# An LSTM whose input part per step comes from DRAM as three bfloat16 rows instead of from SBUF in float32

## The chip, the cores and the metric

The kernel runs on one core of one Trainium2 chip. A core has five engines that run side by side and wait for each other through semaphores: TensorE (PE; its weight loads are listed apart as PEld), VectorE (DVE), ScalarE (ACT), GpSimd (POOL) and SyncE (SP), which here only issues transfers. The metric is the time of one execution on the device, in microseconds (us); lower is better.

## The reference

The input is x, 1250 rows of 512 floats, with 20000 edges (src, dst) between the rows. Two blocks are added to it:

```
x = x + gnn(layernorm(x), src, dst)          # two graph layers with 512x512 weights
x = x + lstm(layernorm(x))                   # one sequence of 1250 steps, hidden size 512

# lstm, for each row t:
combined = concat(x_t, h)                    # 1024
f, i, o  = sigmoid(combined @ W_f + b_f), ...(W_i), ...(W_o)
c        = f * c + i * tanh(combined @ W_c + b_c)
h        = o * tanh(c)
```

The graph layer sums neighbours' rows by dst, scales by the degrees, and multiplies with two weights. The product of x_t with the upper half of the four gate weights does not depend on h, so it can be done for all rows ahead of the recurrence; this is the "input part" of the gates, 2048 numbers per row. The product with h must be done step by step.

## The kernel before, in words

**Stretches.** The 1250 rows are cut into 32 stretches of 40 rows (`P, LEN = 32, 40`), which run side by side. Each stretch starts 90 steps early (`WARM = 90`) with a zero state on the rows that come before it, so that the loop has 130 steps instead of 1250, with 32 rows in each. At the end the kernel compares the state at the end of every stretch with that at the start of the next one, and falls back on a strictly sequential loop (`in_order`) if they differ; with these inputs it doesn't. `EARLY = 3` is how many stretches back the warm-up reaches.

**Tiles.** Rows lie in ten tiles of 128 partitions: tile i holds rows 4i to 4i+3 of all 32 stretches, partition 4p+q being row 4i+q of stretch p. `chunks` and `order` say in which order the tiles are worked on in the graph layers (tiles 8, 9, then 0 to 3, then 4 to 7).

**Stages.** (1) Layer norm, the first linear layer, and the count of the edges into an adjacency matrix, to 205 us. (2) `fast()` starts after a branch: it loads the input half of the gate weights (`load_wx`, 32 KB per partition, in a pool `late_w` at the right end of the SBUF), then `layers()` runs the two graph layers. Their float32 features are written as a sum of three bfloat16 planes (`split`: ACT copies to bfloat16, DVE subtracts, ACT copies the rest, DVE subtracts), which go through TensorE as bfloat16 (line 682). Before the first layer `with_identity` (line 165) scales both layers' weights. (3) `load_wh` loads the recurrent half of the gate weights, then `gate_inputs` (line 497) is called for the ten tiles: DVE normalises the tile's rows (line 499), TensorE transposes them (line 151), ACT copies the transposes (line 156), TensorE does four products of 128x512 (line 505, j = 0 to 3), and DVE adds the bias and writes the result, float32, to SBUF (line 507). `xw_tile(i)` says where: in buffers of the layers that are free by then (`adj`, `planes`, `h`, `base1`). (4) `lstm()` runs the 130 steps.

**A step.** The gates of the 32 stretches lie in two PSUM tiles (s = 0, 1; each has half of the hidden units of every 128-block), with partition 32j+p for block j of stretch p. `open_gates` (line 528) writes the input part into them: for each s and j one product of a selection matrix `sel` with 32 columns and the tile's 128 rows; the columns of `sel` pick row q of every stretch, shifted by e stretches in the warm-up. `add_gates` (line 536) adds the recurrent products, 32 of them, in an order that is written out by hand:

```
for b, s in ((0, 0), (1, 0), (0, 1), (2, 0), (3, 0), (1, 1), (2, 1), (3, 1)):
```

Blocks b = 0, 1 need the state of half 0 (`hT0`), blocks 2, 3 that of half 1. A float32 product is two matmul instructions in the trace, and the four column groups j run side by side on the array. `cell` (line 540) follows for s = 0 and s = 1: three ACT instructions (lines 543, 545, 547), two DVE (549, 550), ACT (552), DVE (553), and a DVE transpose (554) which makes the new `hT` of that half.

**What sets the order of the work.** Pools of buffers and a planner: the planner orders the instructions of each engine, DMA issues on SP and POOL too, from estimated times, and an instruction of a later part of the program can stand ahead of one of an earlier part. In the blocks under `manual_schedule` PE, DVE and ACT keep the written order; SP and POOL stay with the planner. In each engine the order is then fixed, and an instruction that waits holds up all behind it. Buffers of closed pools are used again, and what is written there first waits for the last use before.

**Transfers around the steps.** `x2c` is a copy of the rows in the order of the steps, 40 transfers of 64 KB (line 759, half on SP and half on POOL), in a buffer that is free only after stage 3. In the last 40 steps POOL adds the output of the step to it (line 781), and `store` (line 717) writes it out, in six groups, on SP.

Of the kernel before, what the change touches and what calls it, by code (L numbers as in the profile page):

```python
# [9 lines left out]
F32 = mybir.dt.float32  # L10
F16 = mybir.dt.float16
BF16 = mybir.dt.bfloat16
# [26 lines left out]
def gnn_lstm_kernel(  # L39
# [63 lines left out]
    WARM = 90  # L103
    EARLY = -(-WARM // LEN)

    sel = keep.tile([128, 4, EARLY + P], F32, name="sel")

    def load_rows(i, dst):

# [73 lines left out]
    with ExitStack() as gnn_stack:  # L183
# [14 lines left out]
        with tc.tile_pool(name="prep", bufs=1) as prep, \  # L198
# [209 lines left out]
        def split(pool, t, v, scale):  # L408

            hi, mid, lo = (planes[:, t, i, :] for i in range(3))  # L410
            rest = pool.tile([R, D], F32, name="rest")
            if scale is None:
                nc.scalar.copy(hi, v)
                nc.vector.tensor_sub(rest, v, hi)
            else:
                nc.scalar.activation(hi, v, AF.Copy, scale=scale)
                nc.vector.scalar_tensor_tensor(rest, v, scale, hi,
                                               op0=OP.mult, op1=OP.subtract)
# [8 lines left out]
        with tc.tile_pool(name="deg_ps", bufs=1, space=PSUM) as psD, \  # L427
                tc.tile_pool(name="deg_sb", bufs=2) as sbD:
            most = sbD.tile([R, 1], F32, name="most")
            nc.vector.tensor_reduce(most, S.rearrange("b i r -> b (i r)"),  # L430
                                    mybir.AxisListType.X, OP.max)
            nc.vector.tensor_scalar(most, most, 256.0, None, OP.is_gt)
            count_edges(psD)
            row = sbD.tile([R, 1], F32, name="row")
            nc.vector.tensor_reduce(row, deg, mybir.AxisListType.X, OP.add)
            nc.vector.tensor_sub(row, row, most)
            pn = psD.tile([1, 1], F32, name="total")
            nc.tensor.matmul(pn, row, ones, start=True, stop=True)
            missing = sbD.tile([1, 1], I32, name="missing")
            nc.vector.tensor_scalar(missing, pn, -1.0, float(E), OP.mult, OP.add)  # L440
            degree_norm(gnn)
            for t in order[:AHEAD]:
                split(sbD, t, h[:, t, :], norm[:, t:t + 1])
# [53 lines left out]
        def gate_inputs(t, Wx, bx, psT, psM, dst):  # L497
            y = work.tile([R, D], F32, name="xn")
            nc.vector.tensor_scalar(y, x2[:, t, :], mv2[:, t, 0:1], rstd2[:, t:t + 1],
                                    OP.subtract, OP.mult)  # L500
            yT = transposed(work, psT, y, "xT")
            for j in range(4):
                p = psM.tile([R, G], F32, name="psM")
                for k in range(KD):
                    nc.tensor.matmul(p, yT[:, k, :], Wx[:, k, j, :, :],  # L505
                                     start=(k == 0), stop=(k == KD - 1))
# [84 lines left out]
        def general():  # L591
# [27 lines left out]
            with tc.tile_pool(name="any_w", bufs=1) as anyp, \  # L619
# [27 lines left out]
                            layer_out(t, r)  # L647
                rstd_of(anyp, 0, T)
                for t in range(T):
                    xw = anyp.tile([R, 4, NG, 128], F32, name="any_xw")  # L650
                    gate_inputs(t, Wx, bx, ps, ps, xw)
                    nc.sync.dma_start(in_time(xw_d, t), xw.rearrange("b j g m -> b (j g m)"))
# [5 lines left out]
        def layers():  # L658
            with tc.tile_pool(name="gcn_all", bufs=1) as gcn1, \
# [7 lines left out]
                        for v in (h, base1)]  # L667

                for t in order[AHEAD:]:
                    split(gcn, t, h[:, t, :], norm[:, t:t + 1])  # L670
                for l in range(2):
                    with_identity(w1[l], betas[l], 1.0 - betas[l])
                for l in range(2):
                    if l == 1:
                        load_x_again()
# [1 line left out]
                    for f in range(KD):  # L677
                        ps = [psA.tile([128, 4 * R], F32, name="agg") for c in chunks]
                        for k in order:
                            for pl in range(3):  # L680
                                for (t0, n), p in zip(chunks, ps):
                                    nc.tensor.matmul(  # L682
                                        p[:, :n * R], planes[:, k, pl, f * 128:(f + 1) * 128],
                                        adj[:, k, t0:t0 + n, :].rearrange("b i r -> b (i r)"),
                                        start=(k == order[0] and pl == 0),
                                        stop=(k == order[-1] and pl == 2))
                        for (t0, n), p in zip(chunks, ps):
                            nc.scalar.copy(aT[:, f, t0:t0 + n, :].rearrange("b i r -> b (i r)"),
                                           p[:, :n * R])
                    for t0, n in chunks:  # L690
                        for t in range(t0, t0 + n):
                            r = layer_sum(gcn, l, t, product(psM, aT[:, :, t, :], w1[l]))
                            if l == 0:
                                v = gcn.tile([R, D], F32, name="v")
                                nc.scalar.activation(v, r, AF.Relu, scale=norm[:, t:t + 1])
                                split(gcn, t, v, None)
# [5 lines left out]
        def xw_tile(i):  # L702

            n = order.index(i)
            flat, n = ((adj.rearrange("b a i r -> b (a i r)").bitcast(F32), n) if n < 3 else
                       (planes.rearrange("b t i d -> b (t i d)").bitcast(F32), n - 3) if n < 6 else
                       (h.rearrange("b t d -> b (t d)"), n - 6) if n < 8 else
                       (base1.rearrange("b t d -> b (t d)"), n - 8))
            return flat[:, n * 4 * G:(n + 1) * 4 * G].rearrange("b (j g m) -> b j g m", j=4, g=NG)
# [25 lines left out]
        def lstm(late, Wh):  # L735
# [4 lines left out]

            TOL = 2.0 ** -18
            with tc.tile_pool(name="state", bufs=2) as state, \
                    tc.tile_pool(name="lstm_work", bufs=3) as cells, \
                    tc.tile_pool(name="seq", bufs=1) as seq, \
                    tc.tile_pool(name="ps_g", bufs=3, space=PSUM) as ps_g, \
# [19 lines left out]
                with tc.manual_schedule(engines={mybir.EngineType.PE, mybir.EngineType.DVE,  # L765
# [33 lines left out]
                n_far = nc.values_load(far, min_val=0, max_val=128 * 8 * 31)  # L799
                with tc.If(n_far > 0):  # L800
                    for i in range(T):
                        nc.sync.dma_start(in_time(xw_d, i),
                                          xw_tile(i).rearrange("b j g m -> b (j g m)"))
# [5 lines left out]
        def fast():  # L809
            with ExitStack() as side, ExitStack() as right:  # L810
# [46 lines left out]
```

## Time and profile before

Three runs took 1153.22, 1154.4 and 1156.79 us; the median is 1154.4 us.

| | us |
|---|---|
| the profiled execution, its own time | 1157.43 |
| its span, first to last instruction | 1155.7 |
| stage 1, to the branch | 0 to 205 |
| stage 2, the graph layers | 205 to 416 |
| stage 3, input parts of the gates | 416 to 560 |
| stage 4, 130 steps | 560 to 1146 |
| last comparison and stores | 1146 to 1155.7 |
| PE, DVE, ACT, POOL busy | 1100.8, 466.0, 295.1, 64.4 |
| TensorE clock granted, mean | 0.987 |

Busy time of PE counts matmuls from start to modelled end, so that they overlap; that PE is busy doesn't say that it is the limit. In a list of instructions by time, the brackets give how long the engine had been idle before, and whose result ended that. The chain of work that ended last goes backwards from the last instruction, at each step to what released it or, if it had not waited, to the instruction before it on its own engine.

### The profile page before, as it was taken

The numbers are of one execution on the slowest core, as the hardware profiler recorded it, in microseconds if no ns is written. First come the engines' busy times: TensorE is split into PE (matmuls) and PEld (weight loads), VectorE is DVE, ScalarE is ACT, GpSimd is POOL, SyncE is SP. The second block draws the span as 40 slices with busy tenths as digits, with TensorE's granted clock in tenths as the row PEclk, the third lists the DMA queues.
The fourth block names the chain that finished last, engine by engine and source line by source line (L and its number), as shares of the span: only waits on it lengthen the run. The fifth ranks groups of instructions, "written<-read, shape, count | busy, mean of one in ns | idle before, by whom it ended". The sixth has DMA issues, their size and how long they took to land.

```text
span 1155.7 us, 29252 instructions
## 1 busy us (share of the span) xinstructions
PE 1100.8 (95%) x12396; PEld 573.9 (50%) x12396; DVE 466.0 (40%) x1693; ACT 295.1 (26%) x1204; POOL 64.4 (6%) x123
## 2 busy tenths in 40 slices
PE   2899998799999999999899999999999999999997
PEld 1455544355455444444455555555555555555553
DVE  5956565400500542221244444444444344443444
ACT  2312211421500000000233333333333333333332
POOL 2000000300000041000300000000000000010011
PEclk9999999799999999999999999999999999999999
DMA  8000000800200042000500000000000000001111
GB/s 233 1 1 1 1 1 1 239 20 1 78 12 1 0 89 58 0 1 0 92 3 2 3 2 3 2 3 2 3 2 3 3 3 2 21 2 20 20 20 20
DMA packets 25261, 27.99 MB, mean 24 GB/s; under 512 B 3796, under 2 KB 19517, under 8 KB 25119
## 3 DMA queue, kind: packets, MB, share of 16 engines
q1 hardware_dynamic: 19012, 10.73, 4.4%
q0 software_dynamic: 4288, 12.62, 4.0%
q10 hardware_dynamic: 1819, 2.65, 0.8%
q8 instruction: 100, 1.64, 0.6%
q14 instruction: 42, 0.34, 0.1%
HBM read 20.81 MB, written 2.56 MB: 20 GB/s over the span
## 4 chain that ended last, share of the span: by engine, by line
PE 90%; DVE 4%; DMA 2%; ACT 1%; issue 1%; ACTq 0%; POOL 0%; SPq 0%; DVEq 0%
PE gates L536 40%; PE psM L162 15%; PE psM L505 12%; PE agg L682 11%; PE gates L528 9%; PE acc L302 2%; DMA base<-in_x_dram 2%; DMA bx<-in_L_ffn_b_i_dram 1%; PE psT L151 1%; DVE od L288 1%; DVE ob L286 1%; DVE bnst L139 0%; PE acc L299 0%; DVE S L194 0%; ACTq L112 0%
## 5 line engine op out<-in xcount | busy, mean ns | idle before, releaser
L536 PE MATMUL gates<-Wh,hT 128*32 128x256 f32 x8320 | 481.2, 382 | 3.5 <-DVE hT L554 2.9
L536 PEld LDWEIGHTS gates<-Wh,hT 128*32 128x32 f32 x8320 | 244.4, 109 | 229.8 <-DVE hT L554 96.0
L549 DVE TENSOR_TENSOR pr<-sg,cg 128x128 f32<-128x128 f32 x260 | 70.6, 272 | 223.4 <-ACT sg L545 222.8
L682 PE MATMUL agg<-adj,planes 128*128 128x256 bf16 x720 | 135.6, 353 | 9.2 <-ACT planes L419 8.2
L505 PE MATMUL psM<-Wx,xT 128*128 128x512 f32 x320 | 138.7, 594 | 1.5 <-ACT xT L156 1.5
L543 ACT ACTIVATE cg<-gates 128x64 f32<-128x64 f32 x260 | 58.2, 224 | 245.0 <-PE gates L536 240.7
L682 PEld LDWEIGHTS <-planes 128*128 128x128 bf16 x720 | 71.8, 100 | 72.8 <-ACT planes L419 8.8
L552 ACT ACTIVATE th<-cg 128x64 f32<-128x64 f32 x260 | 66.6, 256 | 138.5 <-DVE cg L550 138.5
L505 PEld LDWEIGHTS psM<-Wx,xT 128*128 128x128 f32 x320 | 60.4, 190 | 76.8 <-issue 74.1
L553 DVE TENSOR_TENSOR hh<-so,th 128x64 f32<-128x64 f32 x260 | 58.5, 225 | 86.3 <-ACT th L552 86.3
L554 DVE STREAM_TRANSPOSE hT<-hh 128x64 f32<-128x64 f32 x260 | 63.8, 245 | 27.9 <-DVE hh L553 0.9
L162 PE MATMUL psM<-w,hT 128*128 128x512 f32 x160 | 70.9, 596 | 0.0
L545 ACT ACTIVATE sg<-gates 128x128 f32<-128x128 f32 x260 | 70.5, 271 | 0.2
L550 DVE TENSOR_TENSOR cg<-pr 128x64 f32<-128x64 f32 x260 | 58.4, 225 | 8.9
L547 ACT ACTIVATE so<-gates 128x64 f32<-128x64 f32 x260 | 59.8, 230 | 0.0
L302 PE MATMUL acc<-od,ob 125*128 125x400 f16 (+22 forms) x360 | 48.0, 260 | 10.4 <-DVE od L288 9.6
L288 DVE TENSOR_SCALAR od<-ids,key 125x820 f16<-125x820 f16 (+42 forms) x160 | 55.4, 346 | 0.0
L156 ACT COPY xT<-psT 128x512 f32<-128x512 f32 x20 | 11.2, 587 | 171.9 <-PE psT L151 152.7
L781 POOL TENSOR_TENSOR x2c<-x2c,hh 128x128 f32<-128x128 f32 x40 | 18.3, 458 | 557.2 <-DVE hh L553 557.2
L162 PEld LDWEIGHTS psM<-w,hT 128*128 128x128 f32 x160 | 29.7, 190 | 34.0 <-issue 33.0
L286 DVE TENSOR_SCALAR ob<-ids,low 125x128 f16<-125x128 f16 x160 | 39.4, 246 | 17.7 <-PE acc L302 17.4
L302 PEld LDWEIGHTS <-ob 125*128 125x128 f16 x360 | 29.7, 98 | 32.9 <-issue 12.9
(155 smaller groups left out, 719.2 us busy)
## 6 DMA issues: line engine op xcount, KB each, us to landing
w<-in_L_gnn_w_dram POOLq DMA_DIRECT2D x4, 1024.0 KB, 12.2
x2c<-x SPq DMA_DIRECT2D x20, 64.0 KB, 5.7
x2c<-x POOLq DMA_DIRECT2D x20, 64.0 KB, 5.2
fcw<-in_L_gnn_fc_w_dram POOLq DMA_DIRECT2D x1, 1024.0 KB, 7.7
out_dram<-x2c SPq DMA_DIRECT2D x12, 64.0 KB, 2.0
out_dram<-x2c SPq DMA_DIRECT2D x12, 60.0 KB
base<-in_x_dram SPq DMA_DIRECT2D x5, 128.0 KB, 6.2
base<-in_x_dram ACTq DMA_DIRECT2D x5, 128.0 KB, 8.3
```

The costliest lines, as they stand in the source:

```text
L162: nc.tensor.matmul(p, lT[:, k, :], rhs[:, k, :], start=(k == 0), stop=(k == KD - 1))
L288: nc.vector.tensor_scalar(od[:, :(hi - lo) * T], ids[:, :(hi - lo) * T], float(lo * T), key[:, c:c + 1], OP.add, OP.is_equal)
L302: nc.tensor.matmul(blocks[i][:, (d0 - i * BW) * T:(d1 - i * BW) * T], ob, od[:, (d0 - lo) * T:(d1 - lo) * T], start=False, stop=last)
L505: nc.tensor.matmul(p, yT[:, k, :], Wx[:, k, j, :, :], start=(k == 0), stop=(k == KD - 1))
L528: nc.tensor.matmul(ps[s][32 * j:32 * (j + 1), :, :], lhs(j), rhs(j, s), start=True, stop=False)
L536: nc.tensor.matmul(ps[s][32 * j:32 * (j + 1), :, :], hT[b // 2][:, b % 2, :], Wh[:, b, j, :, 64 * s:64 * (s + 1)], start=False, stop=(b == 3))
L545: nc.scalar.activation(sg, p[:, 0:2, :], AF.Sigmoid)
L547: nc.scalar.activation(so, p[:, 2, :], AF.Sigmoid)
L549: nc.vector.tensor_mul(pr, sg, cg)
L552: nc.scalar.activation(th, cg[:, 0, :], AF.Tanh)
L554: nc.vector.transpose(hT.rearrange("p b c -> p (b c)"), hh[:, m])
L682: nc.tensor.matmul(p[:, :n * R], planes[:, k, pl, f * 128:(f + 1) * 128], adj[:, k, t0:t0 + n, :].rearrange("b i r -> b (i r)"), start=(k ...
```

## The change

The input parts no longer stay in SBUF. In stage 3 each of them is split into three bfloat16 planes that add up to it, and the planes go to DRAM, laid out by step: for every step, one row per stretch and plane. At each step one transfer brings the 32 stretches x 3 planes = 96 rows of 2048 bfloat16 numbers back, into one of five buffers, and a selection matrix of 96 rows and 32 columns, bfloat16, adds the three planes up on TensorE. The shift by stretches in the warm-up is now in the address in DRAM; rows ahead of the first stretch are zeros, written once.

```diff
-    sel = keep.tile([128, 4, EARLY + P], F32, name="sel")
+    sel = keep.tile([3 * P, P], BF16, name="sel")
+    sel_f = keep.tile([3 * P, P], F32, name="sel_f")
+    ident3 = ident[:3 * P, :3 * P].rearrange("r (p i) -> r i p", i=3)
+    nc.vector.tensor_add(sel_f, ident3[:, 0, :], ident3[:, 1, :])
+    nc.vector.tensor_add(sel, sel_f, ident3[:, 2, :])
...
-            nc.gpsimd.memset(sel, 0.0)
-            nc.gpsimd.tensor_copy(sel[:, :, EARLY:], ident.rearrange("b (p q) -> b q p", q=4))
...
-        chunks = [(8, 2), (0, 4), (4, 4)]
+        def split_input(pool, t, v, scale=None):
+            rest = v if scale is None else pool.tile([R, D], F32, name="rest")
+            split(v, rest, *(planes[:, t, i, :] for i in range(3)), scale=scale)
+
+        chunks = [(6, 4), (0, 4), (4, 2)]
...
+        xp_d = dram.tile([LEN, EARLY + P, 3, 4 * G], BF16, name="xp_d")
...
-                nc.vector.tensor_add(dst[:, j, :, :].rearrange("b g m -> b (g m)"), p,
-                                     bx[:, j, :, :].rearrange("p g m -> p (g m)"))
+                put(j, p, bx[:, j, :, :].rearrange("p g m -> p (g m)"))
...
-                for l in range(2):
-                    with_identity(w1[l], betas[l], 1.0 - betas[l])
...
+                        if f == 1:
+                            with_identity(w1[l], betas[l], 1.0 - betas[l])
...
-        def open_step(ps_g, n):
-
-            i, q, e = n % LEN // 4, n % 4, -(n // LEN)
-            return open_gates(ps_g, lambda j: sel[:, q, EARLY - e:EARLY - e + P],
-                              lambda j, s: xw_tile(i)[:, j, :, 64 * s:64 * (s + 1)])
+        def put_planes(pl, j, p, b):
+            v = v_bufs[:, j, :]
+            nc.vector.tensor_add(v, p, b)
+            split(v, v, *(pl[:, i, j * G:(j + 1) * G] for i in range(3)))
+
+        def open_step(load, ps_g, n):
+
+            xs = load.tile([3 * P, 4, NG, 128], BF16, name="xs")
+            nc.sync.dma_start(
+                xs.rearrange("r j g m -> r (j g m)"),
+                bass.AP(tensor=xp_d.tensor,
+                        offset=xp_d.offset + (n % LEN * (EARLY + P) + EARLY + n // LEN) * 12 * G,
+                        ap=[[4 * G, 3 * P], [1, 4 * G]]))
+            return open_gates(ps_g, lambda j: sel, lambda j, s: xs[:, j, :, 64 * s:64 * (s + 1)])
...
             with tc.tile_pool(name="state", bufs=2) as state, \
+                    tc.tile_pool(name="load", bufs=5) as load, \
...
-                x2c = seq.tile([128, T, 4, 128], F32, name="x2c")
+                x2c = base1.rearrange("b t (q m) -> b t q m", q=4)
...
-                        ps = open_step(ps_g, n)
+                        ps = open_step(load, ps_g, n)
...
+                nc.gpsimd.memset(zeros, 0.0)
+                zero_steps(zeros)
...
-                    for t in order:
-                        gate_inputs(t, Wx, bx, psT, psM, xw_tile(t))
+                    for n in range(T):
+
+                        t = (-WARM % LEN // 4 + n) % T
+                        pl = pl_bufs[:, n % 2, :, :]
+                        gate_inputs(t, Wx, bx, psT, psM, lambda j, p, b: put_planes(pl, j, p, b))
+                        nc.sync.dma_start(tile_steps(t), pl.rearrange("b i g -> b (i g)"))
```

`tile_steps(t)` is the part of `xp_d` that holds the four steps of tile t, and `zero_steps` writes the zeros, 120 rows of 6144 numbers, on POOL's queue. The planes are built in two buffers in turn, in the memory of `planes`; the four float32 buffers of `put_planes` and the zeros lie in that of `adj`. Since the input parts have left `base1`, `x2c` is put there. The tiles of stage 3 come in the order of the steps: the first step, 90 before the start, is row 30 of a stretch and so of tile 7, and the order is 7, 8, 9, 0 to 6. Each layer's weight is now scaled inside the layer, after the second of four blocks of the neighbour sum. The planes of the graph layers are split as before, in place where no scale is needed. The fallback loop adds the three planes up again before it starts.

More of the change, by code (lines that the diff above doesn't have):

```diff
@@ L406, in degree_norm, with split @@
             nc.vector.tensor_scalar(norm9, norm, 1.0 - ALPHA, None, OP.mult)
-        def split(pool, t, v, scale):
-            hi, mid, lo = (planes[:, t, i, :] for i in range(3))
-            rest = pool.tile([R, D], F32, name="rest")
+        def split(v, rest, hi, mid, lo, scale=None):
             if scale is None:
@@ L416, in split @@
                 nc.scalar.activation(hi, v, AF.Copy, scale=scale)
-                nc.vector.scalar_tensor_tensor(rest, v, scale, hi,
-                                               op0=OP.mult, op1=OP.subtract)
+                nc.vector.scalar_tensor_tensor(rest, v, scale, hi, op0=OP.mult, op1=OP.subtract)
             nc.scalar.copy(mid, rest)
             nc.vector.tensor_sub(lo, rest, mid)
-        chunks = [(8, 2), (0, 4), (4, 4)]
+        def split_input(pool, t, v, scale=None):
+            rest = v if scale is None else pool.tile([R, D], F32, name="rest")
+            split(v, rest, *(planes[:, t, i, :] for i in range(3)), scale=scale)
+        chunks = [(6, 4), (0, 4), (4, 2)]
         order = [t for t0, n in chunks for t in range(t0, t0 + n)]
@@ L442, in gnn_lstm_kernel @@
             for t in order[:AHEAD]:
-                split(sbD, t, h[:, t, :], norm[:, t:t + 1])
+                split_input(sbD, t, h[:, t, :], norm[:, t:t + 1])
             n_missing = nc.values_load(missing, min_val=0, max_val=E + R)
@@ L495, in rstd_of, with gate_inputs @@
             nc.vector.tensor_copy(rstd2[:, t0:t0 + n], r)
-        def gate_inputs(t, Wx, bx, psT, psM, dst):
+        def gate_inputs(t, Wx, bx, psT, psM, put):
             y = work.tile([R, D], F32, name="xn")
@@ L649, in general @@
                 for t in range(T):
-                    xw = anyp.tile([R, 4, NG, 128], F32, name="any_xw")
-                    gate_inputs(t, Wx, bx, ps, ps, xw)
-                    nc.sync.dma_start(in_time(xw_d, t), xw.rearrange("b j g m -> b (j g m)"))
+                    xw = anyp.tile([R, 4, G], F32, name="any_xw")
+                    gate_inputs(t, Wx, bx, ps, ps,
+                                lambda j, p, b: nc.vector.tensor_add(xw[:, j, :], p, b))
+                    nc.sync.dma_start(in_time(xw_d, t), xw.rearrange("b j g -> b (j g)"))
                     nc.sync.dma_start(in_time(x2_d, t), x2[:, t, :])
@@ L669, in layers @@
                 for t in order[AHEAD:]:
-                    split(gcn, t, h[:, t, :], norm[:, t:t + 1])
-                for l in range(2):
-                    with_identity(w1[l], betas[l], 1.0 - betas[l])
+                    split_input(gcn, t, h[:, t, :], norm[:, t:t + 1])
                 for l in range(2):
@@ L695, in layers @@
                                 nc.scalar.activation(v, r, AF.Relu, scale=norm[:, t:t + 1])
-                                split(gcn, t, v, None)
+                                split_input(gcn, t, v)
                             else:
@@ L700, in layers, with tile_steps, zero_steps @@
                             rstd_of(gcn1, t0, n)
[L702 to L709, printed above, removed]
-        def open_step(ps_g, n):
-            i, q, e = n % LEN // 4, n % 4, -(n // LEN)
-            return open_gates(ps_g, lambda j: sel[:, q, EARLY - e:EARLY - e + P],
-                              lambda j, s: xw_tile(i)[:, j, :, 64 * s:64 * (s + 1)])
+        def tile_steps(i):
+            return bass.AP(tensor=xp_d.tensor,
+                           offset=xp_d.offset + (4 * i * (EARLY + P) + EARLY) * 12 * G,
+                           ap=[[12 * G, P], [(EARLY + P) * 12 * G, 4], [1, 12 * G]])
+        def zero_steps(rows):
+            nc.gpsimd.dma_start(
+                bass.AP(tensor=xp_d.tensor, offset=xp_d.offset,
+                        ap=[[(EARLY + P) * 12 * G, LEN], [12 * G, EARLY], [1, 12 * G]]), rows)
+        v_bufs = adj.rearrange("b a i r -> b (a i r)")[:, :8 * G].bitcast(F32).rearrange(
+            "b (n g) -> b n g", g=G)
+        zeros = adj.rearrange("b a i r -> b (a i r)")[:EARLY * LEN, 8 * G:20 * G]
+        pl_bufs = planes.rearrange("b t i d -> b (t i d)")[:, :24 * G].rearrange(
+            "b (n i g) -> b n i g", n=2, i=3)
+        def put_planes(pl, j, p, b):
[10 more added lines that the diff above has]
+            return open_gates(ps_g, lambda j: sel, lambda j, s: xs[:, j, :, 64 * s:64 * (s + 1)])
         def store(x2c, n0, n1):
@@ L801, in lstm @@
                     for i in range(T):
-                        nc.sync.dma_start(in_time(xw_d, i),
-                                          xw_tile(i).rearrange("b j g m -> b (j g m)"))
+                        pl = pl_bufs[:, i % 2, :, :]
+                        nc.sync.dma_start(pl.rearrange("b i g -> b (i g)"), tile_steps(i))
+                        v = h.rearrange("b t d -> b (t d)")[:, :4 * G]
+                        nc.vector.tensor_add(v, pl[:, 0, :], pl[:, 1, :])
+                        nc.vector.tensor_add(v, v, pl[:, 2, :])
+                        nc.sync.dma_start(in_time(xw_d, i), v)
                         nc.gpsimd.dma_start(in_time(x2_d, i), x2[:, i, :])
```

## The prediction

> **What bounds the kernel now.** I read the chain of waits first, because it seems to answer the question.
>
> ```profile
> PE 90%; DVE 4%; DMA 2%; ACT 1%; issue 1%; ACTq 0%; POOL 0%; SPq 0%; DVEq 0%
> PE gates L536 40%; PE psM L162 15%; PE psM L505 12%; PE agg L682 11%; PE gates L528 9%; PE acc L302 2%; DMA base<-in_x_dram 2%; DMA bx<-in_L_ffn_b_i_dram 1%; PE psT L151 1%; DVE od L288 1%; DVE ob L286 1%; DVE bnst L139 0%; PE acc L299 0%;
> ```
>
> Line 528, the selection that the change makes cheaper, stands there with 9%. By this view TensorE is the limit of the steps. But the chain follows an engine back whenever it finds no long wait on it, so I looked next at busy time by stage (columns: length, then busy us and instructions of PE, PEld, DVE, ACT, POOL, then clock, DMA share, GB/s).
>
> ```profile
> 416.00:560.00 144.00, 142.15 (x352) 64.12 (x352) 33.41 (x58) 4.92 (x10) 17.41 (x32) 1.00 0.14 29
> 560.00:570.00 10.00, 7.30 (x132) 4.78 (x136) 2.36 (x13) 4.09 (x10) 8.74 (x16) 1.00 0.79 155
> 570.00:966.00 396.00, 395.18 (x7096) 212.08 (x7086) 164.64 (x709) 135.89 (x711) 2.19 (x5) 1.00 0.03 5
> ```
>
> Stage 3 has much room on DVE and ACT; the steps look full of PE. So I took one step apart, in the order of time (start, length, engine, line; in brackets the idle time before and its end):
>
> ```profile
> 803.25 0.23 ACT L543 ACTIVATE cg<-gates 128x64 f32<-128x64 f32 x1 [1.86 <-PE gates L536]
> ...
> 804.24 1.05 PE L528 MATMUL gates<-planes,sel 128*32 128x256 f32 x16
> 804.26 0.26 ACT L552 ACTIVATE th<-cg 128x64 f32<-128x64 f32 x1 [0.50 <-DVE cg L550]
> 804.55 0.22 ACT L543 ACTIVATE cg<-gates 128x64 f32<-128x64 f32 x1
> ...
> 804.88 0.24 DVE L554 STREAM_TRANSPOSE hT<-hh 128x64 f32<-128x64 f32 x1
> ...
> 805.18 1.02 PEld L536 LDWEIGHTS gates<-Wh,hT 128*32 128x32 f32 x24 [0.38 <-DVE hT L554]
> 805.18 3.70 PE L536 MATMUL gates<-Wh,hT 128*32 128x256 f32 x64
> ...
> 806.21 0.25 DVE L554 STREAM_TRANSPOSE hT<-hh 128x64 f32<-128x64 f32 x1
> 806.51 1.89 PEld L536 LDWEIGHTS gates<-Wh,hT 128*32 128x32 f32 x40 [0.31 <-DVE hT L554]
> ```
>
> The two PEld brackets decide. At 805.18 the weights of (0,0) are the `hT0` that DVE finished at 804.88 + 0.24 = 805.12; at 806.51 those of (2,0) are the `hT1` finished at 806.46. In both cases PE starts 0.05 us after DVE. The single matmuls in the trace come in groups of four column blocks every 215.6 ns; 20 groups (4 of line 528, 16 of line 536) make 4.31 us, and the step takes 4.453 us (median distance of the `hT0` transposes). The remaining 0.14 us are PE waiting: 0.078 before (0,0), 0.010 before (2,0), and twice 0.024 for a weight load that nothing hides.
>
> The loop that sets 4.453: (2,0) starts at 802.06 (one step before 806.51); ten groups later (3,1) ends and `cell` of half 1 starts at 804.55 (2.49 us); its `hT1` is ready at 806.46 (1.91); the next (2,0) starts at 806.51 (0.05). Line 528 is not in this loop. The loop through `hT0` is 0.01 us shorter and doesn't hold it either: half 0 is finished by (3,0), before line 528 is reached. Line 528 fills a gap of 0.86 + 0.08 us in which PE would wait.
>
> **What the Trainium skill says.** TensorE: Matmul & The Clock Gate, Back-to-back issue gap: N/2.4 + 2.5 ns between warm matmuls, 109 ns for 256 columns. The trace's 215.6 ns for a float32 group is twice that, so the bfloat16 form with one instruction in place of two may halve each group again. Same page, "Wait — 56ns, not 53.3ns?": starts are never closer than about 25 ns; the trace has no case that dense. DMA: Bandwidth & Descriptors, Anatomy of one DMA: about 2.0 us + bytes/436 GB/s, a fit for transfers that GpSimd issues; no load of this size stands alone in the trace, but the stores of 128 KB landed in 2.3 us, which agrees.
>
> **The change part by part** (against the profiled span of 1155.7; its own time, 1157.43, is 3.0 above the median of 1154.4, so I add the sum to the median).
>
> *Line 528.* Before, 16 instructions, 0.86 us a step. After, 8 instructions of one pass: 2 groups x 109 ns = 0.22 us at best; if they come no closer than today's 54 ns each, 0.43; if a switch between types drains the array, up to 0.86. On the path: 130 x 0. The gap hides all three; PE waits longer for `hT0`. Were the gap not there, it would be worth 130 x 0.43 to 0.65 = 56 to 84 us.
>
> *A load per step.* 96 x 4 KB = 393 KB on SP. Packets of 4 KB took 214 ns (205 to 231 us) to 315 ns (560 to 576 us) per DMA engine; 6 packets on each of 16 are 1.3 to 1.9 us. With the page's fixed 2.0 us and this, 3.3 to 3.9, or 2.9 by its formula; I take 3.3. A step lasts 4.45 and five buffers give four steps, 17.8 us, of lead, so steady loads are hidden. Queued with them on SP are the stores: the group at 1039.9 has eight issues of about 0.43 us, 3.4 us in all; 3.4 + 3.3 < 17.8. That SP isn't kept in program order is seen there too: four stores of single rows went out 27 us ahead of that group, in which they are written.
>
> *Stage 3.* Per j, DVE gains two subtractions (0.69 each, as line 414) and ACT two casts (0.62, as line 413). Per tile DVE has 4 x 3 x 0.69 + 0.54 = 8.8 us and ACT 4 x 2 x 0.62 + 0.54 = 5.5, against 14.45 of PE (28.9 for two). Even strictly one after the other, add to last subtraction, a j takes 0.72 + 2.71 = 3.43 us (the graph layer's split runs from 286.26 to 288.97 without its gap), which is PE's 3.43. PE keeps its pace: 0. The tile's store, 1.57 MB, is 24 packets x 0.22 to 0.31 = 5 to 7.5 us per engine, under 14.45. Clearing the zeros is 12.7 us of POOL at most (0.29 us for 140 elements, times 44), after its `Wh` issues end at 437.8; its store and 20 `x2c` issues of 0.55 us follow long before 560. The 20 on SP (15 us) fit in its gaps between tile stores.
>
> *The seam at 560.* Here cover is missing. Before, the last add ended at 560.05, line 528 started at 560.20 and line 536 at 561.06. After, the step buffers lie where `Wx` and `bx` lay (by the sizes in the code 165 KB per partition are in use to the left, 20 KB are the buffers, 40 KB the weights to the right; `x2c`, of the same size and in that place before, could not start until 560.08 either), so the first load can go when that last add ends, 560.05, and lands 3.3 us later, 563.4 (2.9: 563.0; 4.5: 564.6). With 0.1 of wait and 0.43 of line 528, line 536 starts at 563.9. Behind the last add DVE also has two subtractions with two casts between, 2.75 us, to 562.8, and only then the memsets of `hT` (0.3): 563.1, so a faster load would gain little. Loss 563.9 - 561.06 = 2.9; bounds 2.0 and 4.5.
>
> *Moved or small.* `with_identity` goes behind the second block; ACT and DVE are nearly idle there (DVE waited 47 us at 284.7), without that cover 2 x 2.9 us. Two small adds on DVE for `sel` at the start: hidden behind the load of x that ends at 24.7, else 0.3. POOL loses 0.7 there, gaining nothing for the same reason. The new order of chunks has the same 720 matmuls; the wait for line 416 after the branch (215.6, 219.6), behind the weight loads, stays; it may move by 4 us either way, as nothing in the change fixes it.
>
> Sum: 0 + 0 + 0 + 2.9 = +2.9: 1157.3.
>
> **Rivals.**
> *PE is the limit after all* (the chain's 90%). Then 130 x 0.43 to 0.65 come off: 1070 to 1098. Against it: both PEld brackets. A step that drops under 4.3 us would prove it.
> *The first load stands behind the last tile's store,* on SP or because the planner takes `xp_d` as one piece. The store can go at 562.8, needs 0.7 + 5 to 7.5 + 2, then the load 3.3: line 536 at 574.3 to 576.8, +13 to +16: 1168 to 1170; if only queued behind it, some 2 less. This ends slower; it decides as soon as the load is issued later than 561.5. For it: program order. Against: the planner puts DVE's line 499 of stage 3 ahead of the last tile of the layers (392.6), and graph planes were read (205.8) before later ones of the same buffer were written.
> *Loads come late around stores.* If SP keeps a store that waits for its step ahead of the next loads, each of five groups costs 3.4 + 3.3 - the slack, some 4 to 5 us: 1177 to 1183. Against: the single-row stores above.
> *ACT casts stand ahead of the transposes' copies* (line 156, PE waits only 0.29 us for them now): up to 2.7 us at five pairs of tiles, 1158 to 1171.
>
> **How the numbers follow.** Measurement can't tell less than 0.3%, 3.5 us, from nothing: 1150.9 to 1157.9. Likeliest, seam alone: 59 in 100, own range 1154 to 1160; 36 of them within the bound, 23 above. PE the limit: 6, faster. The fetch after the branch 4 us better: 4, faster. Load behind the store: 15, slower. Stores: 7, slower. Copies: 9, 3 of them same. Faster 0.10, same 0.39, slower 0.51. The range 1152 to 1171 leaves out the first rival, the stores, and an edge of the fetch case.
>
> **What would show it.** Right: line 528 with half the instructions or less busy time, `hT0` distance still 4.45, PE idle before (0,0) some 0.5 to 0.7 us longer, waiting on line 554; SP's first step load near 560, the first line 528 at 563 to 564; stage 3 still 144 us. Wrong: a step under 4.3, PE waits for `xs` inside the loop, idle PE within stage 3, or a first load after 563.

## The result, and the profile after

The changed kernel takes 1156.99 us (median of 12 runs, 1154.85 to 1159.98); the kernel before, in runs taken beside them, 1154.43 (12 runs). The ratio is 1.002, with a 95% interval of 1.0009 to 1.0032: about 2.6 us more, which is inside the 0.3% that the prediction called no change, though the interval leaves out 1: a small loss, and a real one. The profiled execution took 1157.69 us, with a span of 1155.9.

First the chain of waits of the kernel after, the view that had shown PE 90% and line 528 with 9%:

```profile
PE 67%; DVE 16%; ACT 9%; issue 4%; DMA 3%; POOL 0%; DVEq 0%; ACTq 0%; SPq 0%
PE gates L540 28%; PE psM L166 15%; PE agg L685 11%; PE psM L510 10%; DVE pr L553 3%; ACT th L556 3%; DVE hT L558 3%; DVE hh L557 3%; DVE cg L554 3%; ACT cg L547 3%; PE acc L303 2%; ACT sg L549 2%; DMA base<-in_x_dram 2%; DMA bx<-in_L_ffn_b_i_dram 1%; PE psT L155 1%
```

The selection has left the chain, 9% of it, and the time has not moved. The steps appear now as what they were before too: a loop from PE through ACT and DVE and back. Before, the longest wait of PE in the step that was taken apart was 0.078 us, and the chain ran along PE; now it is 0.54, and the chain follows it to DVE.

The busy time by stage of the kernel after (columns: length, then busy us and instructions of PE, PEld, DVE, ACT, POOL, then clock, DMA share, GB/s):

```profile
413.40:557.40 144.00, 142.11 (x352) 64.07 (x352) 85.65 (x136) 52.78 (x88) 21.62 (x40) 1.00 0.41 136
557.40:567.40 10.00, 5.85 (x80) 3.14 (x80) 2.09 (x8) 4.42 (x7) 0.00 (x0) 0.83 0.89 283
570.00:966.00 396.00, 347.49 (x6388) 187.03 (x6380) 164.56 (x708) 135.94 (x711) 0.00 (x0) 1.00 0.31 92
```

Stage 3 keeps PE as full as before, 142.11 of 144 us; DVE's 33 us have become 86 and ACT's 5 have become 53. In the third row PE is busy for 347 us instead of 395 in the same 396 us, and DVE and ACT do as much as before: the same number of steps, with more idle PE in each. The second row is the seam, with a granted clock of 0.83.

One step of the kernel after, in the order of time:

```profile
803.02 0.22 ACT L547 ACTIVATE cg<-gates 128x64 f32<-128x64 f32 x1 [1.86 <-PE gates L540]
...
804.01 0.40 PE L532 MATMUL gates<-xs,sel 96*32 96x256 bf16 x8
...
804.65 0.25 DVE L558 STREAM_TRANSPOSE hT<-hh 128x64 f32<-128x64 f32 x1
...
804.95 1.02 PEld L540 LDWEIGHTS gates<-Wh,hT 128*32 128x32 f32 x24 [0.83 <-DVE hT L558]
804.96 3.70 PE L540 MATMUL gates<-Wh,hT 128*32 128x256 f32 x64 [0.54 <-DVE hT L558]
...
806.28 1.89 PEld L540 LDWEIGHTS gates<-Wh,hT 128*32 128x32 f32 x40 [0.31 <-DVE hT L558]
```

The selection takes 0.40 us (before: 1.05 us by the same view), and PE then stands for 0.54 us until `hT0` is there. From this weight load of (2,0), 806.28, back to the one before, 801.82, are 4.46 us; the median distance of the `hT0` transposes is 4.461 us, against 4.454 before.

Where the spans differ (differences of the two traces' records, in us):

| stretch | before | after | difference |
|---|---|---|---|
| start to first matmul of stage 3 | 415.98 | 413.34 | -2.64 |
| stage 3, first to last matmul | 143.34 | 143.34 | 0 |
| to the first recurrent matmul (line 536/540) | 1.74 | 4.57 | +2.83 |
| to the first `hT0` | 6.73 | 7.04 | +0.31 |
| to the last `hT1` | 581.28 | 581.02 | -0.26 |
| to the end of the span | 6.59 | 6.60 | +0.01 |

The loss is the seam; the first row hides it in this pair of executions, and the second experiment shows what that row is worth. The seam in the trace of the kernel after:

```profile
557.44 0.82 SPq L734 DMA_DIRECT2D xs<-xp_d  x2
...
559.51 1.28 ACT L547 ACT_TABLE_LOAD   x1
559.53 0.69 DVE L418 TENSOR_TENSOR planes<-adj,planes 128x512 bf16<-128x512 f32 x1 [0.68 <-ACT planes L417]
560.25 0.53 SPq L854 DMA_DIRECT2D xp_d<-planes  x1
...
560.92 0.40 PE L532 MATMUL gates<-xs,sel 96*32 96x256 bf16 x8 [4.23 <-DMA xs<-xp_d]
...
561.25 5.29 PE L540 MATMUL gates<-Wh,hT 128*32 128x256 f32 x64
```

In the kernel before the same place looked so:

```profile
560.20 1.07 PE L528 MATMUL gates<-base,sel 128*32 128x256 f32 x16 [0.88 <-DVE base L507]
561.06 3.66 PE L536 MATMUL gates<-Wh,hT 128*32 128x256 f32 x64
563.52 1.28 ACT L543 ACT_TABLE_LOAD   x1 [31.49 <-PE gates L536]
564.81 0.22 ACT L543 ACTIVATE cg<-gates 128x64 f32<-128x64 f32 x1
```

In the kernel after, PE's last matmul of stage 3 ends at 556.68. The first load goes at 557.44, ahead of the last tile's store at 560.25, and PE waits 4.23 us for it. Two things here were not in the prediction: the first step's 64 matmuls take 5.29 us instead of 3.66, and the first of ACT's two table loads (1.28 us each) is done while PE waits, where before it stood between PE and the cell, at 563.52. A table load brings into ACT the tables of the functions that follow.

### The profile page after: what moved, and what is told of

Its sections match the earlier page's. It is cut to its first block, busy times and chain, and to the rows that moved or that the text cites. A ratio compares the mean times of both kernels' runs of the same rounds, so it can differ in the third digit from the quotient of the medians.

```text
span 1155.9 us, 27516 instructions
## 1 busy us (share of the span) xinstructions
PE 1025.9 (89%) x11340; PEld 535.2 (46%) x11356; DVE 519.3 (45%) x1775; ACT 344.4 (30%) x1284; POOL 69.8 (6%) x123
## 4 chain that ended last, share of the span: by engine, by line
PE 67%; DVE 16%; ACT 9%; issue 4%; DMA 3%; POOL 0%; DVEq 0%; ACTq 0%; SPq 0%
PE gates L540 28%; PE psM L166 15%; PE agg L685 11%; PE psM L510 10%; DVE pr L553 3%; ACT th L556 3%; DVE hT L558 3%; DVE hh L557 3%; DVE cg L554 3%; ACT cg L547 3%; PE acc L303 2%; ACT sg L549 2%; DMA base<-in_x_dram 2%; DMA bx<-in_L_ffn_b_i_dram 1%; PE psT L155 1%
## 5 line engine op out<-in xcount | busy, mean ns | idle before, releaser
L685 PE MATMUL agg<-adj,planes 128*128 128x512 bf16 (+1 forms) x704 | 134.6, 352 | 10.0 <-ACT planes L415 7.2
L806 POOL TENSOR_TENSOR base<-base,hh 128x128 f32<-128x128 f32 x40 | 18.4, 461 | 693.0 <-issue 533.4
L532 PE MATMUL gates<-xs,sel 96*32 96x256 bf16 x1040 | 52.5, 272 | 4.2 <-DMA xs<-xp_d 4.2
```

The source lines that it names most:

```text
L685: nc.tensor.matmul(p[:, :n * R], planes[:, k, pl, f * 128:(f + 1) * 128], adj[:, k, t0:t0 + n, :].rearrange("b i r -> b (i r)"), start=(k ...
```

## The experiments

Theory: the step is set by the loop through `hT1`, with PE waiting in it, so a cheaper selection is worth nothing; the loss is the first load's wait at the seam. Rival: TensorE's own work sets the step, or some of it, and something given back elsewhere hides the gain.

**The selection left out of the kernel before.** The gates then lack the input part; only the time is of use here.

```diff
-                        ps = open_step(ps_g, n)
-                        add_gates(ps, hT, Wh)
+                        ps = [ps_g.tile([128, NG, 64], F32, name=f"gates{s}") for s in range(2)]
+                        add_gates(ps, hT, Wh, opens=True)
```

> The kernel before, without line 528: the input part is left out of the gates, the first recurrent product of each half opens the sum. My theory, a step is bound by the loop through hT1, in which line 528 isn't: the distance of the hT0 transposes stays at 4.45 us (4.43 to 4.47), PE idles some 0.9 us before the first recurrent product, the time stays within 4 us of before. The rival, PE is the limit: the step loses 0.86 us and falls to about 3.6, the whole 112 us.

Measured: 1157.17 us (one run), and a median `hT0` distance of 4.500 us, 0.046 longer than with the selection. The step in its trace:

```profile
801.35 0.24 DVE L554 STREAM_TRANSPOSE hT<-hh 128x64 f32<-128x64 f32 x1
...
801.71 1.05 PEld L536 LDWEIGHTS gates<-Wh,hT 128*32 128x32 f32 x24 [1.29 <-ACT so L547]
801.74 3.66 PE L536 MATMUL gates<-Wh,hT 128*32 128x256 f32 x64 [0.84 <-DVE hT L554]
```

With 0.86 us of PE's work gone from every step PE waits 0.84 us where it waited 0.078, and the rival is refuted: it wanted 3.6 us a step. The 0.046 have a likely place: `hT0` is ready at 801.59 and (0,0) starts 0.15 us later, not 0.06, and the weight load now waits for ACT as well, which frees the PSUM tile; before, line 528 had done that wait.

**The kernel before once more, unchanged.**

> The kernel before once more, for a second profile of it. In the changed kernel's profile the graph layers' first neighbour sum started 1.9 us earlier (203.9 against 205.8), which hides most of the loss at the seam there. If that is scatter between executions, this profile's start differs from 205.8 by a like amount (1 to 3 us) with the seam unchanged: from the end of the last product of stage 3 to the first hT0 8.5 us. If it comes from the change, 205.8 is repeated within 0.3 us.

Measured: 1154.78 us. Stage 3 starts at 412.96 us instead of 415.98, with the same code; the seam, from the end of stage 3 to the first `hT0`, is 8.47 us both times; the step 4.459 instead of 4.454 us. So the -2.64 in the first row of the table and the 0.007 us between the two kernels' steps are no larger than what executions of one kernel differ by.

**The step buffers in memory that is free early.** `h` has no reader left in stage 3, so the first loads need not wait for its end.

```diff
-            xs = load.tile([3 * P, 4, NG, 128], BF16, name="xs")
+            xs = h.rearrange("b t d -> b (t d)").bitcast(BF16)[
+                :3 * P, (n + WARM) % 5 * 4 * G:((n + WARM) % 5 + 1) * 4 * G].rearrange(
+                    "r (j g m) -> r j g m", j=4, g=NG)
```

> The changed kernel with the five step buffers in the memory of h, which is free from the end of the graph layers, so that the first loads can go before stage 3 ends. My theory, the loss is the wait for the first load and what follows from PE's idle time: the first line 532 comes within 1 us of the end of stage 3 in place of 4.2, its recurrent products run at full clock, and the time falls by 3 to 5 us against the changed kernel, to 0 to 2 us below before. Rival, the loss lies in the 130 loads or in stage 3: the time stays at 1.002 of before.

Measured: 1153.69 us (14 runs), 3.3 us less than the change as it was made (3.85 when each is set against the kernel before of its own batch); against the kernel before the ratio is 0.999, interval 0.9978 to 1.0002. The seam in its trace:

```profile
557.45 0.40 PE L532 MATMUL gates<-h,sel 96*32 96x256 bf16 x8 [0.78 <-DVE adj L728]
557.79 3.66 PE L540 MATMUL gates<-Wh,hT 128*32 128x256 f32 x64
...
564.07 5.16 PE L540 MATMUL gates<-Wh,hT 128*32 128x256 f32 x64 [2.40 <-DVE hT L558]
```

The wait for the load is gone, the first recurrent matmul comes 1.12 us after stage 3 instead of 4.57, and the first `hT0` 7.10 instead of 11.61. That the loss lies in this wait is shown. The gain of 4.5 us at the first `hT0` is partly given back one step later: PE had stood for 2.40 us, and the second step's matmuls are slow instead of the first's.

**The loop of the kernel before, shortened.** On ACT the sigmoid of f and i goes ahead of the tanh of g; on DVE one column of each new `hT` is set to zero ahead of the cell.

```diff
-            nc.scalar.activation(cg[:, 1, :], p[:, 3, :], AF.Tanh)
             sg = pool.tile([128, 2, 64], F32, name=f"sg{s}")
             nc.scalar.activation(sg, p[:, 0:2, :], AF.Sigmoid)
+            nc.scalar.activation(cg[:, 1, :], p[:, 3, :], AF.Tanh)
...
                         hT = [state.tile([128, 2, 32], F32, name=f"hT{s}") for s in range(2)]
+                        for s in range(2):
+                            nc.vector.memset(hT[s][:, 0, 0:1], 0.0)
```

> The kernel before with two small edits in the cell that shorten the loop without touching PE's work: the sigmoid of f and i stands ahead of the tanh of the candidate on ACT, and a DVE memset of one column of each new hT ahead of the cell takes over its wait for PE. If this drops the semaphore instruction ahead of the first ACT instruction (0.06 us) and that ahead of the hT transpose (0.07), the loop falls to 4.32 us, but PE needs 4.31 and two bare weight loads of 0.024, so that the step falls to 4.36 to 4.39: 8 to 12 us off. If the step isn't bound by the loop, or the two instructions cost nothing, the time stays.

Measured: 1132.91 us (5 runs), ratio 0.982, interval 0.9805 to 0.9835: two edits that take nothing from PE, and add two DVE instructions a step, save 22 us, where 8 to 12 were expected. The median step is 4.321 us. The medians of the steps account for 17 of the 22; from the first `hT0` to the last `hT1` the trace has 560.70 us instead of 581.28, 20.6 less, and at the seam the first `hT0` comes 1.4 sooner. The rest is in the steps that are longer than the median, which add some 2 us in all instead of 5; why was not looked into. Its busy time over 570 to 966 us:

```profile
570.00:966.00 396.00, 396.00 (x7344) 224.37 (x7340) 176.32 (x920) 140.63 (x736) 2.25 (x5) 1.00 0.02 4
```

No idle time of PE is left, and the step is near the 20 x 0.2156 = 4.31 us of its matmuls: of the runs here, this is the one in which TensorE is the limit. The expectation counted on weight loads that nothing hides, which a step of 4.321 us leaves no room for.

**The same two edits on the kernel after,** with its own buffers, and then with those in `h`.

> The kernel after with the same two edits that shortened the loop of the kernel before (sigmoid of f and i ahead of the tanh of g; one column of each new hT set to zero ahead of the cell). TensorE's own work in a step is now 16 x 0.2156 + 0.40 = 3.85 us instead of 4.31. Theory: the loop through hT1 sets the step, and it is itself about 4.31 us long when shortened (in the shortened kernel before: (2,0) to the sigmoid 2.41, to hT1 ready 1.81, to the weight load and (2,0) 0.10). So the step stays near 4.31 us, PE waits 0.3 to 0.4 us ahead of (0,0), and the time is 1157.0 - 130 x 0.145 - 1.3 (one table load less at the seam) = 1136 to 1138, that is the shortened kernel before plus the seam's 3 us. Rival: the loop of the shortened kernel before was shorter than TensorE's 4.31 and hidden behind it; then the step falls under 4.27 us here and the time under 1131, and the change pays as soon as the loop is short.

> The same as the last, with the step buffers in memory that is free long before the steps, which takes the seam's loss away. Theory: 3.3 us less than it, 1133 to 1135, level with the shortened kernel before (1132.9). Rival (loop shorter than TensorE's need): below 1128.

Measured: 1133.74 us (5 runs; ratio to the kernel before 0.9814, interval 0.9795 to 0.9833) and 1127.29 us (5 runs; 0.9774, 0.9754 to 0.9793). The steps have medians of 4.291 and 4.292 us, between the 4.31 of the theory and the 4.27 of its rival: the shortened loop is 4.29 us long, 0.02 less than TensorE's floor with the old selection. To that extent the rival was right, and the time of the second run is the one that it named (below 1128). In the second of them PE waits again:

```profile
805.15 2.15 PE L540 MATMUL gates<-Wh,hT 128*32 128x256 f32 x36 [0.41 <-DVE hT L558]
```

So the cheap selection is worth 3 to 4 us once the loop is short, by the medians (4.321 - 4.292) x 130 = 3.8, by the stretch from the first `hT0` to the last `hT1` 560.70 - 557.73 = 3.0, and then it hits the loop again. With the seam's loss still in, the change brings nothing that can be seen (ratios 0.982 and 0.9814). With the early buffers it is the fastest version here, 27 us under the kernel before in the same batch. The two edits alone gave 22 of them. The median of the second is 6.5 us below the first; their profiles give 4.6 of that at the seam (the first `hT0` 5.68 instead of 10.24 us after stage 3), and in the profiles most of the other difference lies before stage 3, which begins at 414.74 and at 411.30 us, like the scatter seen above.

**Each of the two edits alone,** on the kernel before (the diffs are the two halves of the one above).

> The kernel before with only the sigmoid of f and i put ahead of the tanh of g. Theory: in half 1 the product starts 0.43 us instead of 0.50 us after the cell's first activation, 0.07 us a step, and one table load of 1.28 us less at the seam: 1154.4 - 130 x 0.07 - 1.3 = 1144; step 4.38 to 4.39 us. If the swap gives the table load alone: 1153, step 4.45.

> The kernel before with only one column of each new hT set to zero ahead of the cell, so that the transpose no longer waits for the matmuls that read the old one. Theory: 0.06 to 0.07 us between the product and the transpose go, in every step: 1154.4 - 130 x 0.065 = 1146; step 4.39 us. If that gap is no wait that can be taken away: 1154 or, with two more memsets on DVE, 1160.

Measured: the swap 1146.37 us (4 runs; ratio 0.9917, 0.9889 to 0.9944), step 4.396; the zeroed column 1140.86 us (4 runs; 0.9881, 0.986 to 0.9902), step 4.352. They save 0.06 and 0.10 us a step, and 0.16 together, which is the step of the shortened kernel after (4.461 - 0.16 = 4.30, measured 4.29). The product and the transpose of half 1, first before and then with the zeroed column:

```profile
805.88 0.23 DVE L553 TENSOR_TENSOR hh<-so,th 128x64 f32<-128x64 f32 x1 [0.32 <-ACT th L552]
806.21 0.25 DVE L554 STREAM_TRANSPOSE hT<-hh 128x64 f32<-128x64 f32 x1
```

```profile
802.79 0.22 DVE L553 TENSOR_TENSOR hh<-so,th 128x64 f32<-128x64 f32 x1 [0.32 <-ACT th L552]
803.05 0.25 DVE L554 STREAM_TRANSPOSE hT<-hh 128x64 f32<-128x64 f32 x1
```

The zeroed column gives more than I expected: the transpose comes 0.26 instead of 0.33 us after the start of its product in both halves, and the first one's delay had also held up the second half's product `pr` (0.43 instead of 0.50 us after the cell's first activation). The swap's gain lies elsewhere than I expected: the first activation starts 0.06 us sooner after PE (the bracket was 1.86 in the step shown in the prediction), and `pr` comes no sooner after it:

```profile
806.03 0.28 ACT L544 ACTIVATE sg<-gates 128x128 f32<-128x128 f32 x1 [1.80 <-PE gates L536]
```

**TensorE kept at work over the seam** of the kernel after, by matmuls that nobody reads.

```diff
+                    warm = ps_c.tile([128, NG, 64], F32, name="warm")
+                    for i in range(14):
+                        for j in range(4):
+                            nc.tensor.matmul(warm[32 * j:32 * (j + 1), :, :], Wh[:, i % 4, j, 0, 0:32],
+                                             Wh[:, i % 4, j, :, 0:64], start=True, stop=True)
```

> The kernel after with 14 groups of matmuls between stage 3 and the first step, whose result nobody reads (14 x 0.2156 = 3.0 us), so that TensorE doesn't stand still while the first load is under way. If its 4.2 us of rest made the 64 matmuls of line 540 in the first step slow (5.29 us instead of 3.66), they take about 3.7 us here, the first hT0 comes 1.6 us earlier after the end of stage 3 (10.0 instead of 11.6), and the time is 1155.4. If the slow first step is due to the load's transfer or to the first use of the weights, it stays at 5.3 us and the time at 1157.

Measured: 1156.51 us (20 runs; ratio 1.0017, 1.0009 to 1.0026), which the medians can't tell from the kernel after. The first step in its trace:

```profile
560.95 3.42 PE L540 MATMUL gates<-Wh,hT 128*32 128x256 f32 x59
...
563.35 0.23 ACT L547 ACTIVATE cg<-gates 128x64 f32<-128x64 f32 x1 [3.64 <-PE gates L540]
```

The granted clock from 560 to 565 us, in the kernel after and here:

```profile
560.00:565.00 5.00, 4.08 (x48) 2.22 (x52) 0.22 (x1) 0.80 (x1) 0.00 (x0) 0.66 1.02 346
560.00:565.00 5.00, 4.80 (x98) 2.83 (x86) 0.00 (x0) 1.62 (x3) 0.00 (x0) 1.00 0.98 333
```

The 59 matmuls here take 3.42 us, at the pace of every later step, and the clock is 1.00 instead of 0.66, with the same load before: it is the rest that makes TensorE slow, not the transfer. On the first use of the weights this run says nothing, since the extra matmuls use them too; the early buffers rule it out, as their first step took 3.66 us. From the first recurrent matmul, 560.54, to the first activation are 2.81 us instead of 4.07. But stage 3's last matmul came 0.6 us later among the extra work, and the load with it, and the first recurrent matmul started 4.19 instead of 3.81 us after the load's issue. Of 1.26 us, 0.3 are left at the first `hT0`, counted from the start of stage 3; the first `hT0` comes 10.73 us after stage 3, not the 10.0 that were expected.

**The selection of the kernel after, issued twice.**

```diff
-            for s in range(2):
+            for i, s in enumerate((0, 0, 1, 1)):
...
-                                     start=True, stop=False)
+                                     start=True, stop=(i % 2 == 0))
```

> The kernel after with every matmul of line 532 issued twice; the second result takes the place of the first, so the output is the same. That is 0.40 us more of TensorE in each of 130 steps. Theory (the loop through hT1 sets the step; PE waits 0.54 us ahead of (0,0)): the wait shrinks to some 0.1 us, the step stays 4.46 and the time 1157, at most 1159. If TensorE's own work counts in the step: up to 130 x 0.40 = 52 us more, 1209.

Measured: 1157.54 us (20 runs), 2.9 above the kernel before of its batch, as the change itself is 2.6 above; step 4.457 us. The step in its trace:

```profile
804.70 0.62 PE L532 MATMUL gates<-xs,sel 96*32 96x256 bf16 x16
805.64 2.62 PE L540 MATMUL gates<-Wh,hT 128*32 128x256 f32 x44 [0.32 <-DVE hT L558]
```

Twice the instructions take PE's wait from 0.54 to 0.32 us and the step stays. The added eight cost 0.22 us, not 0.40, so the wait shrank by less than was expected.

## Why the prediction was right

*The step.* Right, and the step of the prediction that decides. It read the loop from single instructions against the chain of waits, which gave PE 90%, and set 130 x 0 for line 528. The step stayed (4.454, 4.461), PE's wait came out at 0.54, that is 0.46 longer than the 0.078 of before, where 0.5 to 0.7 longer was named (its own cost of 0.43 for line 528 would have given 0.43), and neither taking the selection away nor doubling the new one shortened or lengthened the step by more than 0.05 us. What was too simple was to take the 2.49 us from (2,0) to the cell and the 1.91 us of the cell as fixed: the swap takes 0.06 us from the first and the zeroed column 0.10 from the second.

*The price of line 528.* I took 0.43 us, between 0.22 and 0.86. Busy time is 0.40, which holds the drain of the last matmul; what eight more of them cost is 0.22, two groups of 0.11. That is what the Trainium skill (TensorE: Matmul & The Clock Gate, Back-to-back issue gap) states for one pass of 256 columns, 109 ns, and the trace agrees. The two spacings of single matmuls that the prediction weighed against it, 25 ns and 54 ns, were misread: in the steps of both kernels' traces the four column blocks of a group start 6 to 7 ns apart, so the floor of 25 ns between starts does not hold for them, and the 54 is only a quarter of the 215.6. None of this made a difference behind the loop.

*The loads.* Right. Within the steps no PE wait on `xs` appears: line 532 has 4.2 us of idle time ahead of it in 130 steps, all at the seam. The profile of the kernel after gives 3.2 us from issue to landing for the 384 KB loads, as its median, where I had taken 3.3, between 2.9 and 3.9. That is over the 33 of 130 whose landing is on record; two of these, issued at 560.8 and 562.5 right behind the last tile's store, took 8.9 and 10.3 us, and the lead of four steps hid that.

*Stage 3.* Right: 143.34 us both times. DVE's 85.65 us and ACT's 52.78 are close to ten tiles of the 8.8 and 5.5 that the prediction worked out.

*The seam.* Right in place, and in size with some luck: +2.83 us at the first recurrent matmul, where 2.9 was predicted, and 2.6 in the medians. The load went 0.76 us after the last matmul (0.73 was assumed) and ahead of the last store, so the rival that would have cost 13 to 16 us didn't come. Two terms were missing and nearly cancel: TensorE slow after its rest, 5.29 - 3.66 = +1.63 us, and the first table load taken out of the path, -1.28. Together 0.35, and the trace shows 0.31 from there to the first `hT0`; that they nearly cancel was not foreseen. The Trainium skill says that TensorE's clock halves after about 3.4 us of idling (TensorE: Matmul & The Clock Gate, What's actually happening); the wait was 4.23 us, the groups of line 540 then came every 0.43 us instead of 0.2156, and I should have counted it. In the run with the early buffers 2.40 us were already enough, which that figure alone does not explain. One sub-step was wrong: the clearing of `hT` stood ahead of the last subtractions, at 557.63, and not behind them, at the equivalent of 560.5. So "a faster load would gain little" fell, and the early buffers gained 3.3 us.

*The chances.* The change was given 0.51 for slower by more than 0.3% and 0.39 for no change: the outcome with the largest chance did not come. The likeliest single case, +2.9, lies within the bound, and so does the measured 2.6, but only by 0.9 us.

## What to carry to other kernels

An engine that is busy for 99% of a stage need not be its limit. Here 0.14 us of waiting in each step, more than half of it at one place, was the sign of a loop through other engines: put the loop together from single instructions, and take the work away once to see. In this recurrence the cheap gains lay in the hand-overs between engines: look for an instruction whose start waits for two engines. Here the transfers that took the place of data already on chip cost their landing time once (+2.83 us), where their buffer came free last; put such a buffer where nothing late was.

## What the runs showed of the hardware that was not expected

- **Instructions with a second engine to wait for started 0.06 to 0.09 us later.** In three places an instruction started sooner after its last input when it had one engine less to wait for: the transpose on DVE (0.26 instead of 0.33 us after the product, once an earlier memset waits for PE's readers of the old `hT`), the cell's first activation (0.06 us, once it no longer writes a buffer that DVE reads), and in reverse the first weight load in the first experiment (0.15 instead of 0.06 us after `hT0`). The traces show the second wait as an instruction of its own on the same engine: before, 258 semaphore instructions of 21 ns for the 260 transposes, and none with the zeroed column; 262 for the 260 first activations, nearly all of 17 ns, and 4 with the swap; in the first experiment 263 for the weight loads of line 536, nearly all of 51 ns, where there had been 9. The delays are longer than these instructions, and the rest of them stays open. The two edits that follow from it, the table load below among their gains, were worth 22 us of 1154.
- **The order of two functions saves a table load.** With the sigmoid first, ACT loads one table at the seam (1.28 us) instead of two, and with this the first `hT0` comes 7.05 instead of 8.47 us after stage 3. This agrees with the Trainium skill (ScalarE: Activation LUTs, Table sets: the hidden batching unit), by which the set of the sigmoid holds the tanh as well; with the tanh first, another set is loaded for it.
- **A rest of 2.4 to 2.5 us slows TensorE in one place and not in another.** After a rest of 4.23 us 64 matmuls took 5.29 us instead of 3.66, after 3.37 us (in the first experiment) 5.35, and after one of 2.40 us, with the early buffers, 5.16; but in the kernel before, after 2.50 us, they took 3.66, in both of its traces and in that with the zeroed column. What decides between the two was not tried.

```profile
560.61 5.35 PE L536 MATMUL gates<-Wh,hT 128*32 128x256 f32 x64 [3.37 <-DVE hT L554]
568.09 3.66 PE L536 MATMUL gates<-Wh,hT 128*32 128x256 f32 x64 [2.50 <-DVE hT L554]
```
